# A selective scan whose two products change engines: B to GpSimd, C to VectorE

## The chip, the cores and the metric

The kernel runs on one core of a Trainium2 chip. Its time is device microseconds of one launch, from three runs: a median of 15,365.76 us, between 15,361.5 and 15,403.47. All data is float32.

A core has five engines that run side by side and meet at semaphores: TensorE (PE in the profile), VectorE (DVE), ScalarE (ACT), GpSimd (POOL) and SyncE (SP), which here issues nearly all DMA transfers. Each engine works through its own instructions in order. SBUF is the working memory of 128 partitions; PSUM is the smaller memory that PE writes, and that VectorE and ScalarE, but not GpSimd, read and write in this kernel.

## The reference

Sixteen images of 192 channels and 32 x 32 pixels pass through four layers. The change lies in the third, a selective scan in four directions, with 384 inner channels and 16 states for each channel. Cut to what matters:

```python
def step(h, xs_t):
    d_t, u_t, B_t, C_t = xs_t
    dA = jnp.exp(d_t[..., None] * A)                       # decay
    h = h * dA + (d_t * u_t)[..., None] * B_t[:, :, None, :]
    y = jnp.einsum('bkdn,bkn->bkd', h, C_t)                # sum over the 16 states
    return h, y
```

It runs over the 1024 pixels in each direction k: row by row (0), column by column (1), and both from the end (2 and 3). B and C depend on the pixel, the state and the direction, not on the channel.

## The kernel before

**Units.** The first layer runs ahead of everything else and takes some 3,090 us. The rest, class LayersB, is built around one long sequence of scans. A unit is one scan over 128 partitions x 1024 pixels: 16 channels (CW) times 8 states (NBL). So a group of 16 channels takes two units (BLOCKS = 2), a direction 24 groups or 48 units (DIR_UNITS), an image 192 units (UNITS), and the sixteen images 3072.

**Work of a unit.** With dl (the step d, spread over the states), du (d times u), bb (B) and cb (C) in SBUF:

- `inputs_up` (L1849): once a group, ScalarE copies du into a PSUM buffer xt.
- `decay` (L1853): dA = exp(dl x A), ScalarE, into SBUF; three buffers.
- `inputs` (L1860): xt = xt x bb, VectorE, PSUM to PSUM. Both products of a group are made at its first unit.
- `scan` (L1869): h = scan(dA, xt), VectorE, into SBUF; two buffers. For directions 2 and 3 all views are reversed.
- `outputs` (L1881): hc = h x cb, GpSimd, SBUF to SBUF; three buffers. In directions 1 and 3 the pixels of h stand column by column, and hc is written through a turned view, so that it stands row by row: successive elements go 32 words apart.
- `sums` (L1902 to L1911): PE adds hc over the states with the 0/1 matrix sel, into the PSUM bank acc; after eight units `collect` (L1921) copies acc to y on ScalarE.

**Transfers.** SP issues them all: dl and du for a group (`load_group`, L1816), each 512 KB written by reading one row of a channel eight times; bb and cb for a direction (`load_states`, L1809).

**Order.** Everything from the first scan on is issued in an order written out by `scans`: it walks over slots t = 0 to 191 of each image, and in each slot issues a fixed sequence: products and scan of unit t, the product with C of unit t-1, the sums of unit t-2, the copy of du in odd slots, the decay of unit t+2 (AHEAD), and the transfers that `fetch` finds due. In the room left it puts pieces of other work: `front` (the steps dl and du of the next directions: dlh, duh), and two streams of pieces, `prepare` for the next image and `complete` for the one before (layers 1, 2's ends and 3: convolutions on PE, copies and activations on ScalarE, products on GpSimd). Their instructions appear under L800, the helper that meters them.

A planner decides how many pieces fit. It keeps a clock for each engine, advances VectorE's by SLOT in each slot (4.83 us and 2.31 us in turn) and lets another engine run over the slot's end by OVER; ALLOW is the PE and VectorE work that pieces may bring a slot. A piece marked "late" (a Gelu or Tanh, for which ScalarE loads another function table) goes into odd slots only, at their end. `ln_exp` (L72) loads the table for exp and log again.

**Buffers.** [...]In SBUF lie seventeen buffers of 128 x 1024: dA 3, h 2, hc 3, dl 2, du 2, bb 2, cb 3.

Of the kernel before, what the change touches and what calls it, by code (L numbers as in the profile page):

```python
# [20 lines left out]
L = H * W  # L21
# [746 lines left out]
AHEAD = 2  # L768
# [3 lines left out]
SLOT = (4.83, 2.31)  # L772
OWN = {"POOL": 2.36, "SUMS": 0.6, "START": 0.9, "INPUTS": 1.0, "DECAY": 1.15, "COLLECT": 0.57}
ENGINES = ("PE", "ACT", "POOL", "DVE")
ALLOW = {"PE": 2.45, "DVE": 0.3}
OVER = {"PE": (0.8, 1.2), "ACT": (0.0, 1.5), "POOL": (0.5, 1.5)}
# [38 lines left out]
class Stream:  # L815
# [9 lines left out]
    def step(self):  # L825
        self.engine, lag, *mark = next(self.pieces, (None, 0))
        self.ready = self.at + lag
        self.late, self.piped = "late" in mark, "piped" in mark
        if self.late and self.ready % BLOCKS == 0:
            self.ready += 1  # L830
# [7 lines left out]
    def open(self, t):  # L838

        return self.engine and self.ready <= t and not (self.late and t % BLOCKS != BLOCKS - 1)  # L840


class LayersB:
# [135 lines left out]
    def setup_scans(self):  # L979
# [55 lines left out]
        self.dA, self.h, self.hc = ring("dA", 3, [128, L]), ring("h", 2, [128, L]), ring("hc", 3, [128, L])  # L1035
        self.dl, self.du = ring("dl", 2, [128, L]), ring("du", 2, [128, L])
        self.bb, self.cb = ring("bb", BLOCKS, [128, L]), ring("cb", 3, [128, L])
# [3 lines left out]
        self.xt = [self.xp.tile([128, L], F32, name="xt%d" % i) for i in range(2)]  # L1041
# [108 lines left out]
    def prepare(self, b):  # L1150
# [192 lines left out]
        yield "ACT", 0, "late"  # L1343
        xx = xg if b else self.xx
        for g in range(3):
            nc.scalar.activation(xx[:, g, :], xg[:, g, :], AF.Gelu, bias=self.dw2b[:, g : g + 1])
# [8 lines left out]
        for gs in ((0, 1), (2,)):  # L1355
            zs = [self.p4([128, L], "z") for g in gs]
            for g, z in zip(gs, zs):
                for hf in range(2):
                    yield "PE", 3 if g == 2 and hf == 0 else 0
                    p = self.mm()  # L1360
                    matmuls(
                        nc, p, [(wz[:, i, g * 128 : (g + 1) * 128], x[:, i, half(hf)]) for i in range(2)]
                    )
                    yield "ACT", 0
                    nc.scalar.copy(z[:, half(hf)], p)
            yield "ACT", 0, "late"
            for g, z in zip(gs, zs):
                nc.scalar.activation(z, z, AF.Gelu)
                nc.sync.dma_start(self.zd[one(b), g].rearrange("o p l -> p (o l)"), z)
            cx.ln_exp()  # L1370
# [5 lines left out]
    def complete(self, b):  # L1376
# [8 lines left out]
        if last:  # L1385
            for g in range(3):
                nc.sync.dma_start(self.dA[g], self.zd[b, g])
                nc.sync.dma_start(self.xx[:, g, :], self.yd[g])
        wout = self.weight(I["out_projT"].rearrange("(g p) o -> p g o", p=128), [128, 3, C], "wc", 1)
        for hf in range(2):  # L1390
# [28 lines left out]
            zs = [self.dA[g][:, half(hf)] if last else self.slot("cz", [128, HL], "zh", 3) for g in range(3)]  # L1419
# [30 lines left out]
        for k in range(len(todo) + 2):  # L1450
            if k < len(todo):
                n, r, a = todo[k]
                yield "POOL", 0, "piped"
                t = self.c4([P6, L], "t")
                ts.append(t)
                xa = x[:, a, :]
                tr, xr = (q.rearrange("p (h w) -> p h w", w=W) for q in (t, xa))
                if r == 0:
                    products.tensor_mul(t, xa, xa)
                elif r < 8:  # L1460
                    o = 4 * r * W
                    products.tensor_mul(t[:, o:], xa[:, o:], xa[:, : L - o])
                    products.tensor_mul(t[:, :o], xa[:, :o], xa[:, L - o :])
                else:
                    o = 4 * (r - 7)
                    products.tensor_mul(tr[:, :, o:], xr[:, :, o:], xr[:, :, : W - o])
                    products.tensor_mul(tr[:, :, :o], xr[:, :, :o], xr[:, :, W - o :])
            if 1 <= k <= len(todo):
                yield "ACT", 0, "late", "piped"
                nc.scalar.activation(ts[k - 1], ts[k - 1], AF.Tanh, scale=NS**-0.5)  # L1470
            if k >= 2:
                n, r, a = todo[k - 2]
                yield "PE", 0, "piped"
                for q in range(4):
                    nc.tensor.matmul(
                        ps[32 * q : 32 * q + 32, 0:256], lhsT=self.row[:, NS - n : NS - n + 32],
                        rhs=ts[k - 2][:, 256 * q : 256 * q + 256], start=(k == 2), stop=(k == len(todo) + 1),
                    )
# [74 lines left out]
        for hf in range(2):  # L1553
# [57 lines left out]
            yield "ACT", 0, "late"  # L1611
# [24 lines left out]
    def scans(self, b, more, carry):  # L1636
# [9 lines left out]
        for t in range(UNITS):  # L1646
# [3 lines left out]
            for s in (self.before, self.after):  # L1650
                while s.engine == "ACT" and not s.late and self.fits(s, now + SLOT[t % BLOCKS]):
                    self.advance(s)
            if t % BLOCKS == 0:
                for u in range(t, t + BLOCKS):
                    self.inputs(u)
            self.scan(t)
            clock["DVE"] += SLOT[t % BLOCKS]
            end = now + SLOT[t % BLOCKS]
            if t > 0 or carry:
                self.outputs((t - 1) % UNITS, t == 0)  # L1660
                clock["POOL"] += OWN["POOL"]
            if t > 1 or carry:
                self.sums((t - 2) % UNITS)
            if t % BLOCKS == BLOCKS - 1 and (more or t + 1 < UNITS):
                self.inputs_up((t + 1) % UNITS)
                clock["ACT"] += OWN["INPUTS"]
            if more or t + AHEAD < UNITS:
                self.decay((t + AHEAD) % UNITS)
                clock["ACT"] += OWN["DECAY"]
            if t > 1 or carry:  # L1670
                self.collect((t - 2) % UNITS)
            self.fetch(t, more, carry)
# [24 lines left out]
        if not more:  # L1697
            while self.before.engine:
                self.advance(self.before)
            self.outputs(UNITS - 1)  # L1700
            for u in (UNITS - 2, UNITS - 1):
                self.sums(u)
            self.collect(UNITS - 1)

    def fits(self, s, end):
# [4 lines left out]
        if s.engine != "DVE":  # L1710
            end += OVER[s.engine][self.slots % BLOCKS]
# [18 lines left out]
    def begin(self):  # L1730

        for at, piece in self.front(0):
            if at < 0:
                piece()
        for blk in range(BLOCKS):
            self.load_states(self.bb[blk], 0, blk * NBL)
            self.load_states(self.cb[blk], 0, N + blk * NBL)
        self.turns = 0
        for n in range(2):
            self.load_group(n)  # L1740
        for u in range(AHEAD):
            self.decay(u)
        self.inputs_up(0)
        self.load_group(2)
# [66 lines left out]
    def load_group(self, n):  # L1811
# [3 lines left out]
        for t, src in ((self.dl[n % 2], self.dld), (self.du[n % 2], self.dud)):  # L1815
            self.nc.sync.dma_start(  # L1816
                t, src[k, g, i * CW : (i + 1) * CW, :].unsqueeze(1).to_broadcast([CW, NBL, L])
            )

    def fetch(self, t, more, carry):  # L1820


        n, blk = divmod(t, BLOCKS)
        k, at = divmod(t, DIR_UNITS)
        if more or k + 1 < K:


            if at == DIR_UNITS - 2:
                for i in range(BLOCKS):
                    self.load_states(self.bb[i], (k + 1) % K, i * NBL)  # L1830
            if at == DIR_UNITS - 14:
                self.load_states(self.c_of(k + 1, 0), (k + 1) % K, N)
            if at == DIR_UNITS - 1:
                self.load_states(self.c_of(k + 1, 1), (k + 1) % K, N + NBL)

        due = {DIR_UNITS - 3: (), DIR_UNITS - 2: (n - 1,)}.get(at, (n,) if blk == BLOCKS - 1 else ())
        for n in due:
            if more or n + 3 < K * GROUPS:
                self.load_group((n + 3) % (K * GROUPS))

    def c_of(self, k, blk):

        return self.cb[(2 * (self.turns + k) + blk) % 3]

    def inputs_up(self, u):


        n = u // BLOCKS % 2
        self.nc.scalar.copy(self.xt[n], self.du[n])  # L1849

    def decay(self, u):
        n, blk = divmod(u, BLOCKS)
        self.nc.scalar.activation(  # L1853
            self.dA[u % 3], self.dl[n % 2], AF.Exp, scale=self.A[:, blk, n : n + 1]
        )

    def inputs(self, u):

        n, blk = divmod(u, BLOCKS)
        self.nc.vector.tensor_mul(self.xt[(n + 1 + blk) % 2], self.xt[n % 2], self.bb[blk])  # L1860

    def scan(self, u):
        nc = self.nc
        n, blk = divmod(u, BLOCKS)
        k = n // GROUPS
        views = [self.h[u % 2], self.dA[u % 3], self.xt[(n + 1 + blk) % 2]]
        if k >= 2:
            views = [v[:, ::-1] for v in views]
        nc.vector.tensor_tensor_scan(*views, 0.0, op0=ALU.mult, op1=ALU.add)  # L1869

    def outputs(self, u, carried=False):

        n, blk = divmod(u, BLOCKS)

        k = n // GROUPS - K * (carried and u == UNITS - 1)
        views = [self.hc[u % 3], self.h[u % 2], self.c_of(k, blk)]
        if n // GROUPS % 2:
# [3 lines left out]
        self.nc.gpsimd.tensor_mul(*views)  # L1881
# [145 lines left out]
```

## Time and profile before

| what | value |
|---|---|
| median of three runs | 15,365.76 us |
| span of the profiled execution, first to last instruction | 15,414.4 us |
| scan stage in it, first product to end of last scan | 3,310.2 to 15,273.8 us |
| units in the stage | 3072 |

The profiled execution has no time of its own but its span; it lies 48.6 us above the median of the runs. Its page has, for each group of instructions, the line, the engine, output<-inputs with their shapes and the count; then busy time in all and the mean of one in ns; then the idle time of the engine just before them, and which instruction's end ended most of it. A list of waits has one line for each pair of waiter and releaser: the time in all, how often, and the longest. An answer on one tile or line gives the shortest, median and longest of its instructions.

### The profile page before, as it was taken

How to read it: one execution, taken by the hardware profiler on the slowest of the kernel's cores; microseconds unless marked ns; L12 is line 12 of the kernel's file. 1: busy time of each engine (PE TensorE's matmuls, PEld its weight loads, DVE VectorE, ACT ScalarE, POOL GpSimd, SP SyncE). 2: the span in 40 equal slices, each digit the busy share in tenths (PEclk: the TensorE clock that was granted, in tenths of full speed). 3: DMA queues.
4: the chain of work that ended last, by engine and by line, in shares of the span. 5: the costliest groups of instructions: out<-in, count | busy, mean ns of one | idle time of the engine just before them, and what ended most of it. 6: DMA issues, size and time to landing. Idle time of an engine off the chain costs nothing.

```text
span 15414.4 us, 184312 instructions
## 1 busy us (share of the span) xinstructions
PE 12384.4 (80%) x65856; PEld 4810.3 (31%) x65856; DVE 12329.6 (80%) x10115; ACT 9160.4 (59%) x11881; POOL 10313.5 (67%) x6314
## 2 busy tenths in 40 slices
PE   8999999977777778777778787787878787878755
PEld 4444444422222222222222222222222222222212
DVE  4444444469988988888898989898988888889897
ACT  3333333345666666666666666666666666666665
POOL 2222222237787878787887878787878787878785
PEclk9999999978878887888888888887878787878766
DMA  1000000047878777878777777777777777777774
GB/s 30 15 15 15 17 15 15 14 126 185 214 181 212 185 207 182 208 180 210 189 203 191 199 195 198 195 198 194 197 196 194 195 197 199 194 200 186 200 182 129
DMA packets 884782, 2412.09 MB, mean 156 GB/s; under 512 B 146672, under 2 KB 266944, under 8 KB 876224
## 3 DMA queue, kind: packets, MB, share of 16 engines
q1 hardware_dynamic: 871168, 2397.50, 60.8%
q8 instruction: 532, 8.72, 0.2%
q10 hardware_dynamic: 12736, 3.04, 0.1%
q14 instruction: 346, 2.83, 0.1%
HBM read 2019.10 MB, written 364.30 MB: 155 GB/s over the span
## 4 chain that ended last, share of the span: by engine, by line
PE 19%; DVE 16%; POOL 14%; issue 13%; DMA 10%; ACT 7%; SPq 1%; DVEq 0%; POOLq 0%; ACTq 0%
PE mm L800 15%; DVE h L1869 10%; POOL hc L1881 9%; DVE xt L1860 5%; DMA dl<-dld 3%; PE acc L1911 3%; DMA du<-dud 2%; POOL t L800 2%; ACT dA L1853 2%; ACT xt L1849 2%; DMA y<-ydram 1%; DMA yh<-yd 1%; POOL dlh L800 1%; PE acc L1902 1%; DMA yd<-y 1%
## 5 line engine op out<-in xcount | busy, mean ns | idle before, releaser
L1881 POOL TENSOR_TENSOR hc<-h,cb 128x1024 f32<-128x1024 f32 x3072 | 7245.8, 2371 | 2087.6 <-DVE h L1869 1591.0
L1869 DVE TENSOR_TENSOR_SCAN h<-dA,xt 128x1024 f32<-128x1024 f32 x3072 | 6914.6, 2274 | 299.1 <-POOL hc L1881 292.0
L1860 DVE TENSOR_TENSOR xt<-xt,bb 128x1024 f32<-128x1024 f32 x3072 | 3633.2, 1227 | 904.0 <-ACT xt L1849 771.3
L1853 ACT ACTIVATE dA<-dl,A 128x1024 f32<-128x1024 f32 x3072 | 3507.3, 1146 | 810.3 <-DMA dl<-dld 703.4
L1911 PE MATMUL acc<-hc,sel 128*32 128x256 f32 x24576 | 2406.9, 473 | 1717.2 <-POOL hc L1881 1714.3
L800 PE MATMUL mm<-pad,dg 128*128 128x512 f32 (+1 forms) x5580 | 2911.4, 657 | 13.3 <-ACT pad L800 10.6
L1849 ACT COPY xt<-du 128x1024 f32<-128x1024 f32 x1536 | 1557.8, 1014 | 1350.9 <-DVE h L1869 1163.1
L627 POOL TENSOR_TENSOR D<-D,mask 128x256 f32<-128x256 f32 x768 | 542.7, 738 | 2101.1 <-DVE D L624 2101.1
L1911 PEld LDWEIGHTS acc<-hc,sel 128*32 128x32 f32 x24576 | 561.8, 120 | 4060.2 <-POOL hc L1881 2905.2
L800 PEld LDWEIGHTS mm<-pad,dg 128*128 128x128 f32 (+1 forms) x5580 | 999.1, 193 | 1491.8 <-issue 1370.3
L800 PE MATMUL mm<-x,wgt 96*128 96x512 f32 (+1 forms) x1664 | 1053.7, 769 | 146.8 <-ACT o L800 56.4
L1902 PE MATMUL acc<-y,ident 128*128 128x512 f32 x576 | 442.3, 859 | 447.3 <-ACT y L1921 445.9
L800 POOL TENSOR_TENSOR t<-x 96x768 f32<-96x768 f32 (+4 forms) x510 | 647.3, 1289 | 216.9 <-PE mm L800 216.8
L800 PE MATMUL mm<-d,xT 128*96 128x256 f32 x2048 | 567.9, 415 | 5.4 <-ACT o L800 5.0
L800 POOL TENSOR_TENSOR duh<-dlh,xx 128x512 f32<-128x512 f32 x384 | 537.6, 1400 | 30.1
L800 POOL TENSOR_TENSOR dlh<-dlh,e 128x512 f32<-128x512 f32 x384 | 488.5, 1272 | 103.0 <-ACT e L800 101.0
L800 PEld LDWEIGHTS mm<-x,wgt 96*128 96x128 f32 (+1 forms) x1664 | 339.3, 224 | 672.1 <-issue 363.5
L800 PE MATMUL mm<-xd,dtw 12*128 12x512 f32 x768 | 535.6, 783 | 10.3 <-ACT z L800 10.3
L391 PE MATMUL pc<-ypad,w_c 128*64 128x512 f32 (+1 forms) x1152 | 480.3, 664 | 74.2 <-PEq L751 41.5
L624 DVE SCALAR_TENSOR_TENSOR D<-D,s 128x256 f32<-128x256 f32 x768 | 272.0, 416 | 255.2 <-ACT D L620 255.2
L620 ACT ACTIVATE D<-s 128x256 f32<-128x256 f32 x768 | 233.4, 390 | 338.2 <-PE s L613 332.5
L800 PEld LDWEIGHTS mm<-d,xT 128*96 128x96 f32 x2048 | 328.0, 174 | 261.0 <-issue 164.0
(321 smaller groups left out, 14487.7 us busy)
## 6 DMA issues: line engine op xcount, KB each, us to landing
dl<-dld SPq DMA_DIRECT2D x1536, 512.0 KB
du<-dud SPq DMA_DIRECT2D x1536, 512.0 KB
dld<-dlh SPq DMA_DIRECT2D x384, 256.0 KB
dud<-duh SPq DMA_DIRECT2D x384, 256.0 KB
bb<-xdr SPq DMA_DIRECT2D x128, 512.0 KB
cb<-xdr SPq DMA_DIRECT2D x128, 512.0 KB
dg<-dqd SPq DMA_DIRECT2D x270, 192.0 KB
zd<-z SPq DMA_DIRECT2D x48, 512.0 KB
```

The costliest lines, as they stand in the source:

```text
L391: nc.tensor.matmul(p[r, :], lhsT=w_, rhs=v, start=(n == 0), stop=(n == 14))
L620: nc.scalar.activation(d, S[j][:, two], AF.Exp)
L624: nc.vector.scalar_tensor_tensor(d, d, 2.0, S[j][:, 2 * CH :], op0=ALU.min, op1=ALU.mult)
L627: nc.gpsimd.tensor_mul(d, d, mask)
L800: return f(out, *args, **kw)
L1849: self.nc.scalar.copy(self.xt[n], self.du[n])
L1853: self.nc.scalar.activation(self.dA[u % 3], self.dl[n % 2], AF.Exp, scale=self.A[:, blk, n : n + 1])
L1860: self.nc.vector.tensor_mul(self.xt[(n + 1 + blk) % 2], self.xt[n % 2], self.bb[blk])
L1869: nc.vector.tensor_tensor_scan(*views, 0.0, op0=ALU.mult, op1=ALU.add)
L1881: self.nc.gpsimd.tensor_mul(*views)
L1902: nc.tensor.matmul(acc, lhsT=self.cx.ident, rhs=self.y[:, g, half(pair)], start=True, stop=False)
L1911: nc.tensor.matmul(self.acc[rows4(q), q4(s)], lhsT=self.sel[:, m, :], rhs=self.hc[u % 3][:, q4(q)], start=False, stop=(s + m + blk == 3),)
```

## The change

The two products of a unit change places and engines, and with them the memories:

- `inputs`: xs = du x bb on GpSimd, SBUF to SBUF, for unit t+2 in slot t; three buffers xs. The copy of du (`inputs_up`) is gone.
- `decay`: written into PSUM, into one of two buffers h, for unit t+1 in slot t.
- `scan`: in place in PSUM, from h and xs into h.
- `outputs`: hc = h x cb on VectorE, straight behind the scan of the same unit, with the same turned view of hc in directions 1 and 3.
- `sums` and `collect` follow one slot after the scan in place of two.
- `fetch`: dl is loaded two groups ahead and du three, both in even slots; bb has three buffers as cb has, and the loads of a new direction go out 14 and 4 slots (bb) or 14 and 2 (cb) ahead of it.
- `late` is gone: Gelu and Tanh may go into any slot, and each Gelu is a piece of its own.
- Planner: SLOT is 3.55 in every slot; ALLOW for PE 2.7 in place of 2.45; OVER for PE 2.5, ACT 1.0, POOL 2.5.

The seventeen SBUF buffers are now xs 3, hc 3, dl 2, du 3, bb 3, cb 3. The output stage of the last image, which used dA as space, uses xs.

The core of the diff:

```diff
-AHEAD = 2
-SLOT = (4.83, 2.31)
+SLOT = 3.55
+EARLY = 1.3
-ALLOW = {"PE": 2.45, "DVE": 0.3}
-OVER = {"PE": (0.8, 1.2), "ACT": (0.0, 1.5), "POOL": (0.5, 1.5)}
+ALLOW = {"PE": 2.7, "DVE": 0.3}
+OVER = {"PE": 2.5, "ACT": 1.0, "POOL": 2.5}
...
-        self.dA, self.h, self.hc = ring("dA", 3, [128, L]), ring("h", 2, [128, L]), ring("hc", 3, [128, L])
-        self.dl, self.du = ring("dl", 2, [128, L]), ring("du", 2, [128, L])
-        self.bb, self.cb = ring("bb", BLOCKS, [128, L]), ring("cb", 3, [128, L])
+        self.xs, self.hc = ring("xs", 3, [128, L]), ring("hc", 3, [128, L])
+        self.dl, self.du = ring("dl", 2, [128, L]), ring("du", 3, [128, L])
+        self.bb, self.cb = ring("bb", 3, [128, L]), ring("cb", 3, [128, L])
-        self.xt = [self.xp.tile([128, L], F32, name="xt%d" % i) for i in range(2)]
+        self.h = [self.xp.tile([128, L], F32, name="h%d" % i) for i in range(2)]
...
-        yield "ACT", 0, "late"
         xx = xg if b else self.xx
         for g in range(3):
+            yield "ACT", 0
             nc.scalar.activation(xx[:, g, :], xg[:, g, :], AF.Gelu, bias=self.dw2b[:, g : g + 1])
...
                 while s.engine == "ACT" and self.fits(s, now + EARLY - OVER["ACT"]):
                     self.advance(s)
-            if t % BLOCKS == 0:
-                for u in range(t, t + BLOCKS):
-                    self.inputs(u)
+            if more or t + 1 < UNITS:
+                self.decay((t + 1) % UNITS)
+            if more or t + 2 < UNITS:
+                self.inputs(t + 2)
             self.scan(t)
+            self.outputs(t)
             if t > 0 or carry:
-                self.outputs((t - 1) % UNITS, t == 0)
-            if t > 1 or carry:
-                self.sums((t - 2) % UNITS)
-            if t % BLOCKS == BLOCKS - 1 and (more or t + 1 < UNITS):
-                self.inputs_up((t + 1) % UNITS)
-            if more or t + AHEAD < UNITS:
-                self.decay((t + AHEAD) % UNITS)
-            if t > 1 or carry:
-                self.collect((t - 2) % UNITS)
+                self.sums((t - 1) % UNITS)
+                self.collect((t - 1) % UNITS)
...
     def fetch(self, t, more):
         k, at = divmod(t, DIR_UNITS)
         if more or k + 1 < K:
+            for tiles, o, first, second in ((self.bb, 0, 14, 4), (self.cb, N, 14, 2)):
+                for blk, lead in enumerate((first, second)):
+                    if at == DIR_UNITS - lead:
+                        self.load_states(self.turn_of(tiles, k + 1, blk), (k + 1) % K, o + blk * NBL)
+        n, blk = divmod(t, BLOCKS)
+        for tiles, src, lead in ((self.dl, self.dld, 2), (self.du, self.dud, 3)):
+            if blk == 0 and (more or n + lead < K * GROUPS):
+                self.load_group(tiles, src, (n + lead) % (K * GROUPS))
...
     def decay(self, u):
         n, blk = divmod(u, BLOCKS)
         self.nc.scalar.activation(
-            self.dA[u % 3], self.dl[n % 2], AF.Exp, scale=self.A[:, blk, n : n + 1]
+            self.h[u % 2], self.dl[n % 2], AF.Exp, scale=self.A[:, blk, n : n + 1]
         )
     def inputs(self, u):
         n, blk = divmod(u, BLOCKS)
-        self.nc.vector.tensor_mul(self.xt[(n + 1 + blk) % 2], self.xt[n % 2], self.bb[blk])
+        self.nc.gpsimd.tensor_mul(self.xs[u % 3], self.du[n % 3], self.turn_of(self.bb, n // GROUPS, blk))
     def scan(self, u):
+        h, x = self.h[u % 2], self.xs[u % 3]
+        if u // DIR_UNITS >= 2:
+            h, x = h[:, ::-1], x[:, ::-1]
+        self.nc.vector.tensor_tensor_scan(h, h, x, 0.0, op0=ALU.mult, op1=ALU.add)
     def outputs(self, u):
+        k, at = divmod(u, DIR_UNITS)
+        views = [self.hc[u % 3], self.h[u % 2], self.turn_of(self.cb, k, at % BLOCKS)]
+        if k % 2:
             views = [views[0].rearrange("p (h w) -> p w h", w=W)] + [
                 v.rearrange("p (w h) -> p w h", h=H) for v in views[1:]
             ]
-        self.nc.gpsimd.tensor_mul(*views)
+        self.nc.vector.tensor_mul(*views)
```

## The prediction

> **What bounds the kernel now.** I read the page's busy shares and groups first, then the list of waits, then busy time over the scan stage, then the rows that show what an access pattern costs.
>
> ```profile
> span 15414.4 us, 184312 instructions
> PE 12384.4 (80%) x65856; PEld 4810.3 (31%) x65856; DVE 12329.6 (80%) x10115; ACT 9160.4 (59%) x11881; POOL 10313.5 (67%) x6314
> L1881 POOL TENSOR_TENSOR hc<-h,cb 128x1024 f32<-128x1024 f32 x3072 | 7245.8, 2371 | 2087.6 <-DVE h L1869 1591.0
> L1869 DVE TENSOR_TENSOR_SCAN h<-dA,xt 128x1024 f32<-128x1024 f32 x3072 | 6914.6, 2274 | 299.1 <-POOL hc L1881 292.0
> L1860 DVE TENSOR_TENSOR xt<-xt,bb 128x1024 f32<-128x1024 f32 x3072 | 3633.2, 1227 | 904.0 <-ACT xt L1849 771.3
> L1853 ACT ACTIVATE dA<-dl,A 128x1024 f32<-128x1024 f32 x3072 | 3507.3, 1146 | 810.3 <-DMA dl<-dld 703.4
> L1849 ACT COPY xt<-du 128x1024 f32<-128x1024 f32 x1536 | 1557.8, 1014 | 1350.9 <-DVE h L1869 1163.1
> ```
>
> There are 3072 units of scan (16 images, 4 directions, 48 units); each takes one product and one scan on VectorE. The stage runs from the first product at 3310.2 us to the end of the last scan at 15273.8 us: 11,964 us, or 3.89 us a unit. In it:
>
> ```profile
> 3300.00:15280.00 11980.00, 9224.59 (x42538) 3215.64 (x42536) 10738.85 (x7134) 7896.55 (x9517) 9529.57 (x5246) 0.80 0.77 195
> ```
>
> After the length come PE, PEld, VectorE, ScalarE, GpSimd, the clock, DMA share and GB/s. VectorE is busy for 10,739 us (90%), GpSimd 80%, PE 77%, ScalarE 66%. VectorE sets the pace; its idle time is 11,964 - 10,739 = 1,225 us. Whom it waits for, over the same stretch:
>
> ```profile
> DVE xt L1860 <- ACT xt L1849: 771.3, 364, 30.0
> DVE h L1869 <- POOL hc L1881: 292.0, 233, 3.4
> DVE yh L800 <- PE mm L800: 40.7, 16, 5.0
> ```
>
> So 1,225 us is the most that a better order can give; the rest is VectorE's own work.
>
> **Copy and decays.** The 1536 copies of du go: 1,558 us of ScalarE, none of VectorE. What counts is the 771 us that VectorE waited for them. A copy could start when the even scan ended and had to be done when the odd scan ended: slack 2.27 - 1.01 = 1.26 us. Now the decay takes that place, for it writes the h buffer that the product of unit t-1 has just read, and scan t+1 needs it: slack 2.27 + 1.23 - 1.15 = 2.35 us, more where the product is slower. The mean overrun was 771/364 = 2.1 us; some 1.1 us more of slack takes about half of it. Against that, every unit is exposed instead of every second, and behind a late ScalarE stand the decay and the copy of acc, for which VectorE and PE wait. If overruns fall off exponentially with a mean of 2.1 us, the share kept is exp(-1.1/2.1) = 0.6, so 771 us becomes 460 us with the same number of chances and 920 us with twice as many. ScalarE loses 0.5 us of work a unit and the dl transfers get more lead (below), so I take the lower, with 40 us for the waits on PE: **500 us** of idle time, ends 200 and 1,000. The decay itself may be 1.01 (the copy that wrote PSUM) to 1.15 us; VectorE's work covers it, unless it is late.
>
> **Product with B on GpSimd.** 3072 products of the shape, type and memory of L1881, now all contiguous, replace L1881's: 7,246 us, nothing net. It is issued two slots ahead into three buffers, so a GpSimd piece has to run over a whole slot before VectorE notices; I count the 292 us wait as gone. It waits for scan t-1, du and bb; the pieces of the other images (dlh, duh, t, D) queue behind it, and their stores dld and dud on SP.
>
> **Scan in place.** 2.27 us as now. The scan of L1869 reads PSUM and SBUF; no row has a scan that writes PSUM, but L1860 writes PSUM in 1.23 us while L131 does the same work wholly in SBUF in 1.22. Between 0 and 0.03 us a unit (92 us); I take 0.
>
> **Product with C on VectorE.** It takes the place of the product with B, 1.23 us: nothing net where it is contiguous. But in directions 1 and 3, half of the units, it writes hc through a turned view: neighbours in the stream lie 32 words apart. GpSimd hardly notices (median 2360 ns in a direction 0, 2381 in the direction 1 after it):
>
> ```profile
> L1881 POOL TENSOR_TENSOR hc<-h,cb x43: 2339/2360/2389, 7073.4 to 7233.6; 128x1024 f32<-128x1024 f32 x43
> L1881 POOL TENSOR_TENSOR hc<-h,cb x42: 2362/2381/2399, 7261.2 to 7413.5; 128x1024 f32<-128x1024 f32 x42
> ```
>
> No VectorE row in the trace writes so. Two rows are near: ScalarE's copies of xd, alternately contiguous and turned with the same step, and a small reduction of VectorE that reads 96 elements at that step, against one of 4 elements (min/median/max):
>
> ```profile
> L800 ACT COPY xd<-mm x1: 578/578/578, 3283.9 to 3283.9; 44x512 f32<-44x512 f32 x1
> L800 ACT COPY xd<-mm x2: 578/816/1055, 3283.9 to 3284.5; 44x512 f32<-44x512 f32 x2
> ...
> L231 DVE TENSOR_REDUCE row<-ident x1: 315/315/315, 5.1 to 5.1; 128x24 f32<-128x96 f32 x1
> L238 DVE TENSOR_REDUCE rowg<-ident x6: 145/146/146, 5.3 to 5.7; 128x1 f32<-128x4 f32 x6
> ```
>
> ScalarE: (1014 - 578)/512 = 0.85 ns an element contiguous, and (1055 - 578)/512 = 0.93 more turned: 1.78 ns. VectorE reading: (315 - 146)/92 = 1.84 ns. Two engines of different speed end at about 1.8 ns, so I take 1.8 for VectorE's write, against (1227 - 667)/512 = 1.09 contiguous (667 is its 512-wide yh row), or 1.04 at the least: 1024 x 0.75 = **0.77 us** a product, 1536 x 0.77 = 1,183 us. The Trainium skill (Vector Engine (DVE) Microarchitecture Reference, Measured stream behaviour on trn2) speaks against the change: a port keeps its rate only on runs of two adjacent words, and a destination alone costs 1.71 ns an element hopping 4 KiB and 2.50 to 2.51 stepping 24 words, against 1.05. By its ends the product grows by 0.68 or 1.49 us, 1,040 or 2,290 us in all. I keep these as ends, and the rows for the value, as they have the very step.
>
> **Transfers.** Same number and size of dl, du, bb and cb. A load of dl went out behind the decay at the end of an odd slot, for a decay after the next long and short slot: 2 x 1.23 + 2.27 + 2.27 = 7.0 us on. Now it goes out some 1.2 us into an even slot for a decay at the start of the third slot after: 3 x 3.5 - 1.2 = 9.3 us. That is 2.3 us more lead, against 703 us of ScalarE waiting for dl. du has a third buffer; its issue now waits for GpSimd, on SP behind dl, with the stores dld and dud behind both. Loads of bb move from 2 slots ahead to 14 and 4. DMA stands at 77%, so nothing on the path; a gain is within the idle time above.
>
> **Table loads.** Without "late", Gelu and Tanh may go in any slot, one by one. Now there are 197 pairs of loads in the stage (13 an image); at the most 26 an image if each of 18 Tanh and 8 Gelu has its own, 195 pairs more. The row is
>
> ```profile
> L72 ACT ACT_TABLE_LOAD x197 | 252.8, 1283 | 3.5
> ```
>
> and in the order of time the next activation starts 1.29 us after a load, so a pair is 2.57 us and 195 of them 500 us of ScalarE. The Trainium skill (ScalarE: Activation LUTs, What ACT_TABLE_LOAD costs) adds a drain of some 1.38 us, 2.66 us a load: 1,040 us. By either ScalarE stays under 7,897 - 1,558 + 1,040 = 7,380 us of 12,400: off the path, save for single late decays, which the 500 us hold. I take the row.
>
> **Planner.** The larger PE allowance and the wider overruns order pieces differently; they add no work. PE at 77% and GpSimd at 80% have room, but less than ScalarE in a direction 0, where PE is busy 137.5 of 160 us. The end of the program saves one trailing product, some 2 us.
>
> **Sum.** 10,739 + 1,183 + 500 = 12,422 us of stage against 11,964: +458 us. Against the profiled span that is 15,872; the span is 49 us over the median of the runs, so on the median 15,366 + 458 = **15,824 us**, 3.0% slower. The gain in waits is real (725 us) and smaller than the turned write.
>
> **Rivals.**
> - The turned write costs VectorE little, as it costs GpSimd. Then the waits decide: 10,739 + 500 - 11,964 = -725, 14,640 us. It turns at 725/1536 = 0.47 us a product: faster below. Against it: both near rows lie at 0.75 or above. 12%.
> - The turned write costs the skill's 1.49 us: 10,739 + 2,290 + 400 (long slots leave more slack) = 13,429, 16,830 us. For it: 24 words is near 32; against it: the 1.84 ns of VectorE's own read. 18%.
> - ScalarE's one-slot lead fails: its waits on PE and dl reach VectorE nearly every time, idle 1,000 us: 12,922, 16,325 us. For it: ScalarE works in order, and waited 370 us for PE at pad alone. 12%.
> - Loss and gain cancel: 0.68 us and idle 200: 11,984, 15,390 us. 8%, of which half within 0.3%, a quarter on each side.
> - The likeliest, 15,550 to 16,150: 50%.
>
> **How the numbers follow.** A measurement of this kernel can tell about 0.3%, 46 us. Faster: 12 + 2, less 1 for a write between the cases, 13%; within: 4 + 1, 5%; slower: 82%. The range leaves out the first rival, the faster part of the fourth and the far end of the second: 15,340 to 16,950.
>
> **What would show it.** The product on VectorE in two populations, near 1.23 us and 2.0 us, the second in directions 1 and 3 alone, with those directions near 4.3 us a unit and the others near 3.7; scan at 2.27; GpSimd's product at 2.36; VectorE waiting for decays in place of the copy, some 500 us in all; no wait for GpSimd worth naming. Wrong: a single population of products near 1.23 (the first rival), or directions 0 and 2 not under 3.89 us.

## The result and the profile after

The changed kernel takes 15,890.93 us (median of four runs, 15,883.45 to 15,927.11) against 15,363.63 us for the kernel before on the same chip: a ratio of 1.034, 95% interval 1.0325 to 1.0358. It is slower by 3.4%; 15,824 us and 3.0% were forecast.

The page of the kernel after, busy shares and the groups of the scan:

```profile
span 15886.6 us, 183427 instructions
PE 12436.4 (78%) x65856; PEld 4818.6 (30%) x65856; DVE 13489.8 (85%) x10115; ACT 7815.3 (49%) x10376; POOL 10309.3 (65%) x6314
L1837 POOL TENSOR_TENSOR xs<-du,bb 128x1024 f32<-128x1024 f32 x3072 | 7240.9, 2362 | 2549.1 <-DVE h L1844 2313.6
L1844 DVE TENSOR_TENSOR_SCAN h<-h,xs 128x1024 f32<-128x1024 f32 x3072 | 7019.1, 2285 | 216.1 <-ACT h L1830 174.2
L1830 ACT ACTIVATE h<-dl,A 128x1024 f32<-128x1024 f32 x3072 | 3428.6, 1117 | 4601.1 <-DVE hc L1854 4146.4
L1854 DVE TENSOR_TENSOR hc<-h,cb 128x1024 f32<-128x1024 f32 x3072 | 4856.9, 1581 | 319.0 <-DVE h L1844 7.8
```

The scan, the decay and GpSimd's product last about what they did. VectorE's product has a mean of 1,581 ns where the product with B had 1,227. That mean is of two populations, as the answers on the tile hc show, first in a direction 1 or 3, then in a direction 0 or 2 (shortest/median/longest):

```profile
L1854 DVE TENSOR_TENSOR hc<-h,cb x10: 1918/1950/1984, 5879.8 to 5917.5; 128x1024 f32<-128x1024 f32 x10
L1854 DVE TENSOR_TENSOR hc<-h,cb x11: 1223/1225/1225, 6080.5 to 6118.1; 128x1024 f32<-128x1024 f32 x11
```

Over the scan stage, busy times in the order PE, PEld, VectorE, ScalarE, GpSimd, and whom VectorE waits for in it:

```profile
3306.00:15750.00 12444.00, 9274.78 (x42526) 3226.67 (x42526) 11899.54 (x7134) 6540.92 (x8002) 9520.32 (x5244) 0.78 0.74 188
```
```profile
DVE h L1844 <- ACT h L1830: 174.2, 134, 6.7
DVE h L1844 <- POOL xs L1837: 41.4, 8, 31.7
DVE yh L800 <- PE mm L800: 27.0, 11, 5.5
```

The stage grew from 11,964 to 12,444 us. VectorE's busy time grew by 1,161 us and its idle time fell from 1,225 to 544. The wait for ScalarE is down from 771 to 174 us, the wait for GpSimd from 292 to 41. Only some 250 us of the idle time is put down to another engine; the remaining 300 us lie in front of the product with C (319.0 us in its row, 16 of them put down to something), a tenth of a microsecond each time. The forecast has no such term. The order of time shows it, VectorE alone (start, duration), in a turned direction and in a straight one:

```profile
5881.65 2.29 DVE L1844 TENSOR_TENSOR_SCAN h<-h,xs 128x1024 f32<-128x1024 f32 x1
5884.04 1.96 DVE L1854 TENSOR_TENSOR hc<-h,cb 128x1024 f32<-128x1024 f32 x1
5885.82 2.31 DVE L1844 TENSOR_TENSOR_SCAN h<-h,xs 128x1024 f32<-128x1024 f32 x1
...
6081.67 2.29 DVE L1844 TENSOR_TENSOR_SCAN h<-h,xs 128x1024 f32<-128x1024 f32 x1
6084.06 1.23 DVE L1854 TENSOR_TENSOR hc<-h,cb 128x1024 f32<-128x1024 f32 x1
6085.21 2.29 DVE L1844 TENSOR_TENSOR_SCAN h<-h,xs 128x1024 f32<-128x1024 f32 x1
```

and in the kernel before, where VectorE waits for no other engine (two instructions merged in a line):

```profile
15262.52 4.46 DVE L1869 TENSOR_TENSOR_SCAN h<-dA,xt 128x1024 f32<-128x1024 f32 x2
15267.08 2.37 DVE L1860 TENSOR_TENSOR xt<-xt,bb 128x1024 f32<-128x1024 f32 x2
15269.35 4.46 DVE L1869 TENSOR_TENSOR_SCAN h<-dA,xt 128x1024 f32<-128x1024 f32 x2
```

Before, a pair of units takes 15,269.35 - 15,262.52 = 6.83 us, 3.415 a unit. After, a straight unit takes 6,085.21 - 6,081.67 = 3.54 us, for the product starts 0.1 us after its scan has ended (6,084.06 against 6,081.67 + 2.29), where other instructions start a little before their predecessor's end. The kernel before has this gap too, but once in two units: the first product of a pair starts at 15,267.08, the scan before it ended at 15,262.52 + 4.46 = 15,266.98. That product overwrites the buffer xt that the scan just before it has read, and in the trace a wait on VectorE's own counter stands ahead of it. Of the 904 us of idle time in its row some 791 are put down to something, so about 113 us of such gaps were there before the change, against 300 now.

A turned unit takes 4.17 us: 0.63 us more, not the 0.72 us that the durations differ by, for the next scan starts 0.18 us before a turned product's recorded end and only 0.08 us before a straight one's.

### The profile page after: what moved, and what is told of

It is laid out like the page before. It is cut to its first block, busy times and chain, and to the rows that moved or that the text cites. A ratio compares the mean times of both kernels' runs of the same rounds, so it can differ in the third digit from the quotient of the medians.

```text
span 15886.6 us, 183427 instructions
## 1 busy us (share of the span) xinstructions
PE 12436.4 (78%) x65856; PEld 4818.6 (30%) x65856; DVE 13489.8 (85%) x10115; ACT 7815.3 (49%) x10376; POOL 10309.3 (65%) x6314
## 5 line engine op out<-in xcount | busy, mean ns | idle before, releaser
L1837 POOL TENSOR_TENSOR xs<-du,bb 128x1024 f32<-128x1024 f32 x3072 | 7240.9, 2362 | 2549.1 <-DVE h L1844 2313.6
L1844 DVE TENSOR_TENSOR_SCAN h<-h,xs 128x1024 f32<-128x1024 f32 x3072 | 7019.1, 2285 | 216.1 <-ACT h L1830 174.2
L1830 ACT ACTIVATE h<-dl,A 128x1024 f32<-128x1024 f32 x3072 | 3428.6, 1117 | 4601.1 <-DVE hc L1854 4146.4
L1854 DVE TENSOR_TENSOR hc<-h,cb 128x1024 f32<-128x1024 f32 x3072 | 4856.9, 1581 | 319.0 <-DVE h L1844 7.8
L800 PE MATMUL mm<-x,wgt 96*128 96x512 f32 (+1 forms) x1664 | 1110.4, 803 | 146.4 <-ACT o L800 43.2
L1875 PE MATMUL acc<-y,ident 128*128 128x512 f32 x576 | 407.4, 797 | 82.0 <-ACT y L1894 82.0
L1894 ACT COPY y<-acc 128x512 f32<-128x512 f32 x384 | 224.1, 584 | 317.2 <-PE acc L1884 313.0
```

The costliest lines, as they stand in the source:

```text
L800: return f(out, *args, **kw)
L1830: self.nc.scalar.activation(self.h[u % 2], self.dl[n % 2], AF.Exp, scale=self.A[:, blk, n : n + 1])
L1837: self.nc.gpsimd.tensor_mul(self.xs[u % 3], self.du[n % 3], self.turn_of(self.bb, n // GROUPS, blk))
L1844: self.nc.vector.tensor_tensor_scan(h, h, x, 0.0, op0=ALU.mult, op1=ALU.add)
L1854: self.nc.vector.tensor_mul(*views)
L1875: nc.tensor.matmul(acc, lhsT=self.cx.ident, rhs=self.y[:, g, half(pair)], start=True, stop=False)
```

## The experiments

**The turned write taken away.**

```diff
-        if k % 2:
-            views = [views[0].rearrange("p (h w) -> p w h", w=W)] + [
-                v.rearrange("p (w h) -> p w h", h=H) for v in views[1:]
-            ]
         self.nc.vector.tensor_mul(*views)
```

> The changed kernel, but hc is written straight in all four directions; the turn back to row order is left out, so directions 1 and 3 are summed with their columns unturned. Theory (the turned write costs VectorE 0.71 us a product in 1536 units): the product is 1.23 us everywhere, 1,098 us of VectorE's work go, and 50 to 250 us of waits for ScalarE come, because slots are shorter: 14,850 to 15,050 us, which is faster than the kernel before by 2 to 3.5%. Rival (the new order with one slot's lead for the decay is what costs, and the turned write only fills time in which VectorE would wait): the time falls by less than 500 us, to 15,400 or more, and VectorE waits for decays for over 700 us.

Measured: 15,175.72 us, 0.986 of the kernel before (0.984 to 0.988). That is 715 us less than the changed kernel (the kernel before took 15,389 us beside it, 26 more than beside the changed one). The direction was the theory's, and the rival, which needed 15,400 or more, falls; but the theory's range is missed too, by 126 us. Stage and waits:

```profile
3312.00:15060.00 11748.00, 9110.28 (x42518) 3186.41 (x42518) 10934.64 (x7134) 6520.69 (x8002) 9494.51 (x5243) 0.80 0.78 199
```
```profile
DVE h L1844 <- ACT h L1830: 385.1, 254, 7.7
DVE hc L1850 <- PE acc L1880: 38.8, 28, 3.2
```

VectorE is busy 965 us less than with the turn, 0.63 us for each of the 1536 products, not 0.71: I had taken the difference of the recorded durations. And idle time rose from 544 to 813 us, since shorter slots leave ScalarE less slack. So all of the change but the turned write is worth 11,964 - 11,748 = 216 us of stage, and the turned write takes 696. Those 216 us hold the copy's going, the new order, the planner's new numbers and the earlier loads together; no run parts them.

**The suspected cost doubled.**

```diff
-        if k % 2:
+        if True:
             views = [views[0].rearrange("p (h w) -> p w h", w=W)] + [
```

> The changed kernel with the suspected cost doubled: hc is written turned in all four directions, so directions 0 and 2 are summed with rows and columns exchanged. Theory: 1536 more products of 1.94 us: +1,098 us of VectorE's work, less 50 to 150 us of waits that the longer slots hide: 16,840 to 16,940 us. Rival (the turned write is partly hidden, or the order is what costs): under 16,500 us.

Measured: 16,706.67 us, 1.086 of the kernel before (1.084 to 1.087); 816 us more than the changed kernel. The rival, under 16,500, falls; the theory's range is missed from below, again for the 0.63 us:

```profile
3314.00:16577.00 13263.00, 9529.13 (x42523) 3294.99 (x42526) 12871.38 (x7134) 6553.51 (x8002) 9539.61 (x5244) 0.77 0.69 176
```

| scan stage, us | before | straight | changed | all turned |
|---|---|---|---|---|
| length | 11,964 | 11,748 | 12,444 | 13,263 |
| VectorE busy | 10,739 | 10,935 | 11,900 | 12,871 |
| VectorE idle | 1,225 | 813 | 544 | 392 |
| of it, waiting for ScalarE's copy or decay | 771 | 385 | 174 | 58 |

Two steps of 1536 turned products add 965 and 972 us of busy time. Over these three kernels the cost is linear, and what the longer slots give back is idle time.

**The disputed cost by itself.** For the views, step(t, s) takes elements s words apart, and rows_(t, s) is the same loop over contiguous data.

```diff
+        for _ in REP:
+            nc.vector.tensor_mul(step(out, 32), rows_(h, 32), rows_(cb, 32))
...
+        for _ in REP:
+            nc.vector.tensor_mul(rows_(out, 32), step(h, 32), rows_(cb, 32))
```

> The changed kernel with 64 more instructions behind its end, four of each kind, every engine on its own: products of 1024 elements on VectorE (PSUM times SBUF, into SBUF) whose output steps 1, 2, 4, 8, 16, 24, 32 and 64 words from element to element, or goes in pairs of neighbours 32 words apart; with the PSUM input or the SBUF input turned in place of the output; with a turned output in PSUM; a ScalarE copy straight and turned; a GpSimd product straight and turned. Theory (a port slows where single words follow each other, whatever the step): 1.23 us for step 1 and for the pairs, 1.9 to 2.0 for every step from 2 or 4 on, 1.9 to 2.0 for a turned SBUF input, ScalarE 1.0 and 1.9, GpSimd 2.36 and 2.38. By the figures of the Trainium skill (Vector Engine (DVE) Microarchitecture Reference, Measured stream behaviour on trn2) step 24 should be near 2.6 us and far steps near 1.8. Rival (the memory's banks decide): 32 and 64 words much slower than 8 or 24. Turned PSUM operands: between 1.23 and 2.0 us, not known. The whole takes some 130 us more.

Measured: 15,938.38 us in a single run, 47 us above the changed kernel where some 130 were expected, for the new instructions ran between the last image's pieces. So the engines were not each on its own, though GpSimd stood idle beside all steps from 1 to 64 words. Four instructions of each kind (shortest/median/longest, ns). In order: output steps 1, 2, 4, 24 (1008 elements) and 32 words; pairs 32 words apart; PSUM input turned; SBUF input turned; PSUM output turned; ScalarE's copy straight and turned; GpSimd's product straight and turned:

```profile
L933 DVE TENSOR_TENSOR hc<-h,cb x4: 1203/1216/1225, 15761.5 to 15766.9; 128x1024 f32<-128x1024 f32 x4
L935 DVE TENSOR_TENSOR hc<-h,cb x4: 1224/1224/1225, 15768.1 to 15771.9; 128x1024 f32<-128x1024 f32 x4
L937 DVE TENSOR_TENSOR hc<-h,cb x4: 1970/1984/1992, 15773.2 to 15782.2; 128x1024 f32<-128x1024 f32 x4
L943 DVE TENSOR_TENSOR hc<-h,cb x4: 2502/2558/2562, 15813.2 to 15820.9; 128x1008 f32<-128x1008 f32 x4
L945 DVE TENSOR_TENSOR hc<-h,cb x4: 1883/1940/1948, 15823.5 to 15851.1; 128x1024 f32<-128x1024 f32 x4
L949 DVE TENSOR_TENSOR hc<-h,cb x4: 1214/1223/1225, 15861.0 to 15865.0; 128x1024 f32<-128x1024 f32 x4
L951 DVE TENSOR_TENSOR hc<-h,cb x4: 1215/1224/1225, 15870.9 to 15874.6; 128x1024 f32<-128x1024 f32 x4
L953 DVE TENSOR_TENSOR hc<-h,cb x4: 1943/1947/1951, 15875.9 to 15881.8; 128x1024 f32<-128x1024 f32 x4
L955 DVE TENSOR_TENSOR h<-h,cb x4: 1217/1232/1233, 15883.7 to 15887.5; 128x1024 f32<-128x1024 f32 x4
L957 ACT COPY hc<-h x4: 1001/1012/1012, 15888.8 to 15892.4; 128x1024 f32<-128x1024 f32 x4
L959 ACT COPY hc<-h x4: 1867/1930/1941, 15893.5 to 15903.4; 128x1024 f32<-128x1024 f32 x4
L961 POOL TENSOR_TENSOR hc<-xs,cb x4: 2338/2341/2342, 15905.4 to 15914.1; 128x1024 f32<-128x1024 f32 x4
L963 POOL TENSOR_TENSOR hc<-xs,cb x4: 2363/2365/2382, 15917.1 to 15924.5; 128x1024 f32<-128x1024 f32 x4
```

Every other word is free, pairs of neighbours 32 words apart are free, and from 4 words on single words cost: 2.0 us at 4 and 8 words, 1.9 at 16, 32 and 64, 2.56 at 24 (medians not shown above: 1,996 ns at 8, 1,876 at 16, 1,903 at 64). So the rival of the banks falls: 32 and 64 words are no slower than 8. The Trainium skill's figure for a step of 24 words (Vector Engine (DVE) Microarchitecture Reference, Measured stream behaviour on trn2: 2.50 to 2.51 ns an element) is nearly met, with 2.56 us for 1008 elements or 2.54 ns each. But it does not carry over to 32 words, near as that is, and one number "whatever the step", as I had it, is wrong too. The same turn costs nothing where VectorE reads or writes PSUM. ScalarE pays as VectorE does; GpSimd, at 2.3 ns an element anyway, pays 0.02 us.

**The turn on TensorE.** The summing matmuls read hc in any case; here they read it turned. This kernel computes everything.

```diff
+        hc = self.hc[u % 3]
         for q in range(4):
+            x = hc[:, q4(q)] if k % 2 == 0 else hc.rearrange("p (w h) -> p h w", h=H)[:, 8 * q : 8 * q + 8, :]
             nc.tensor.matmul(
-                self.acc[rows4(q), q4(s)], lhsT=self.sel[:, m, :], rhs=self.hc[u % 3][:, q4(q)],
+                self.acc[rows4(q), q4(s)], lhsT=self.sel[:, m, :], rhs=x,
```

> As the straight kernel, but complete: in directions 1 and 3 PE's summing matmuls read hc turned, 32 words from one column to the next. Theory (only VectorE's and ScalarE's ports pay for single words[...]; a float32 matmul takes 403 ns for 256 columns, 1.57 ns each, and so has little to lose): matmuls of 0.40 to 0.46 us, time within 100 us of the straight kernel, 14,850 to 15,150 us, faster than the kernel before. Rival (PE pays too, 1.8 ns a column on top): 0.85 us a matmul, 4 x 0.45 = 1.8 us more PE work a unit in half of the units, with PE busy three quarters of the time: 15,500 us or more.

Measured: 15,242.94 us, 0.991 of the kernel before (0.989 to 0.994), 67 us above the straight kernel; of the two profiled executions it is 17 us the longer (15,213.2 and 15,196.7). TensorE pays in part: the matmuls of a straight and of a turned direction, then all summing matmuls without the turn and with it,

```profile
L1882 PE MATMUL acc<-hc,sel x124: 379/403/636, 5879.5 to 5936.9; 128*32 128x256 f32 x124
L1882 PE MATMUL acc<-hc,sel x128: 379/607/636, 6080.1 to 6138.9; 128*32 128x256 f32 x128
...
L1880 PE MATMUL acc<-hc,sel 128*32 128x256 f32 x24576 | 2385.8, 468 | 1777.1 <-DVE hc L1850 1761.5
L1882 PE MATMUL acc<-hc,sel 128*32 128x256 f32 x24576 | 2736.6, 526 | 1659.5 <-DVE hc L1850 1646.5
```

take 0.40 and 0.61 us, between the 0.46 of the theory and the 0.85 of the rival. They overlap: 24,576 of 526 ns would be 12.9 ms one after another, and keep PE busy for 2.74 ms. So their busy time grows by only 351 us, and PE's in the whole stage by 200, from 9,110 to 9,310 out of 11,762; other matmuls got shorter, beside a granted clock of 0.82 in place of 0.80. The time is outside the theory's range, as the straight kernel's is, and well under the rival's bound; the distance to the straight kernel is as expected.

**Reading turned from PSUM.**

```diff
-            views = [views[0].rearrange("p (h w) -> p w h", w=W)] + [
-                v.rearrange("p (w h) -> p w h", h=H) for v in views[1:]
-            ]
+            views[1] = views[1].rearrange("p (w h) -> p h w", h=H)
+            views[0], views[2] = (views[i].rearrange("p (h w) -> p h w", w=W) for i in (0, 2))
```

> The changed kernel, but in directions 1 and 3 VectorE reads h turned from PSUM and writes hc straight; C is taken as it lies, unturned, so these directions are summed with C's pixels in column order. Theory (single words cost at SBUF's ports and not at PSUM's, as the products on their own showed: 1.22 us for a turned PSUM input against 1.94 for a turned SBUF output): products of 1.23 us everywhere and the straight kernel's time within 60 us, 15,115 to 15,235. Rival (PSUM's turned read is free only where PE and ScalarE leave PSUM alone): products above 1.4 us, 15,400 or more.

Measured: 15,191.39 us, 0.987 of the kernel before (0.985 to 0.988), all products between 1,223 and 1,227 ns. The theory holds inside the loop too, with PE and ScalarE at work on PSUM. Used for the real sum it would need C in row order, which this kernel does not prepare.

**The product ahead of the scan.** This takes from the straight kernel the product's dependence on the instruction just before it.

```diff
+            self.outputs(t)
             self.scan(t)
-            self.outputs(t)
```

> The straight kernel with the product with C ahead of the scan of its unit in place of behind it: it then multiplies the decays by C and leaves the scan's result out of the output. Every instruction and buffer stays; only the product no longer reads what the instruction just before it wrote. Theory (a VectorE instruction that needs its predecessor's output starts 0.12 us later than one that doesn't: 3.54 us a unit in the straight kernel against 3.415 in the kernel before): 3072 x 0.12 = 370 us less, with up to 100 us of it lost to waits for ScalarE, 14,780 to 14,920 us. Rival (the gap belongs to the scan that writes PSUM in place, or to switching between the two kinds of instruction): within 60 us of the straight kernel's 15,176.

Measured: 14,917.45 us, 0.969 of the kernel before (0.968 to 0.971), 258 us less than the straight kernel. It is just inside the range's upper end, and the trace shows that the theory holds for half of the units only. A direction run forwards, and one run from the end:

```profile
5593.71 2.28 DVE L1844 TENSOR_TENSOR_SCAN h<-h,xs 128x1024 f32<-128x1024 f32 x1
5595.90 1.20 DVE L1850 TENSOR_TENSOR hc<-h,cb 128x1024 f32<-128x1024 f32 x1
5597.03 2.28 DVE L1844 TENSOR_TENSOR_SCAN h<-h,xs 128x1024 f32<-128x1024 f32 x1
...
6080.51 2.30 DVE L1844 TENSOR_TENSOR_SCAN h<-h,xs 128x1024 f32<-128x1024 f32 x1
6082.72 1.21 DVE L1850 TENSOR_TENSOR hc<-h,cb 128x1024 f32<-128x1024 f32 x1
6084.03 2.30 DVE L1844 TENSOR_TENSOR_SCAN h<-h,xs 128x1024 f32<-128x1024 f32 x1
```

From scan to scan it is 5,597.03 - 5,593.71 = 3.32 us forwards and 6,084.03 - 6,080.51 = 3.52 us reversed; the straight kernel had 3.54 in both. Here the product reads the very buffer that the scan behind it overwrites. A forward scan writes in the order in which the product reads; a reversed one writes first what the product reads last. In the program the reversed scans, and only they, carry a wait on VectorE's own counter for the instruction just before; in the straight kernel nearly every product carries one, in the kernel before the first product of each pair. (The scans of the kernel before carry one as well, on a product two instructions back.) With no such wait, one in two units and one in each, a unit takes 3.32, 3.415 and 3.54 us. So the wait for the instruction just before costs some 0.2 us a time. Over 1536 forward units that is 1536 x 0.22 = 338 us, of which 258 reached the time; in the stage the wait for the decay went from 385 to 371 us, that for PE's sum, now in front of the product, from 39 to 79, and the rest is not accounted for.

```profile
3299.00:14782.00 11483.00, 8916.15 (x42530) 3162.82 (x42530) 10758.37 (x7134) 6515.69 (x8005) 9496.04 (x5245) 0.81 0.80 204
```

VectorE's busy time is back at 10,758 us, where the kernel before had 10,739: both carry such a wait in about half of the units. That also says what "busy" held in the straight kernel's 10,935: instructions that no longer overlap at their ends. The rival, no more than 60 us from the straight kernel, falls.

**The kernel before without its copy.** This asks whether the copy alone could have been dropped. du is read from SBUF in the product on VectorE, and is loaded two groups ahead.

```diff
-            if t % BLOCKS == BLOCKS - 1 and (more or t + 1 < UNITS):
-                self.inputs_up((t + 1) % UNITS)
-                clock["ACT"] += OWN["INPUTS"]
...
+        if blk == 0 and (more or t // BLOCKS + 2 < K * GROUPS):
+            self.load_group((t // BLOCKS + 2) % (K * GROUPS), (1,))
...
-        self.nc.vector.tensor_mul(self.xt[(n + 1 + blk) % 2], self.xt[n % 2], self.bb[blk])
+        self.nc.vector.tensor_mul(self.xt[(n + 1 + blk) % 2], self.du[n % 2], self.bb[blk])
```

> The kernel before with one part of the change alone: the copy of du is gone, and VectorE multiplies du by bb straight from SBUF into xt; du is loaded two groups ahead in even slots. Theory (VectorE shares a read path of SBUF with GpSimd, so a product with two SBUF inputs and GpSimd's product, busy 80% of the time, hold each other up; Trainium skill, SBUF — State Buffer, Who interferes with whom): VectorE's product grows from 1.23 to 2 us or more, GpSimd's from 2.37 to 3 or more; 16,500 to 19,000 us. That would be why the change keeps one operand of each VectorE instruction in PSUM. Rival (no such contention, for VectorE's product of two SBUF inputs in the first layer takes 1.22 us): the 771 us of waits for the copy go, 14,600 to 15,000 us.

Measured: 19,399.87 us, 1.261 of the kernel before (1.258 to 1.263), beyond the theory's upper end of 19,000 and far from the rival. The groups of the page, then GpSimd and VectorE in order of time (two products merged in each line):

```profile
L1879 POOL TENSOR_TENSOR hc<-h,cb 128x1024 f32<-128x1024 f32 x3072 | 8514.5, 2785 | 3906.9 <-DVE h L1867 2797.1
L1858 DVE TENSOR_TENSOR xt<-du,bb 128x1024 f32<-128x1024 f32 x3072 | 7097.4, 2353 | 192.3 <-DMA du<-dud 135.0
```
```profile
8004.00 5.63 POOL L1879 TENSOR_TENSOR hc<-h,cb 128x1024 f32<-128x1024 f32 x2
8006.00 4.73 DVE L1858 TENSOR_TENSOR xt<-du,bb 128x1024 f32<-128x1024 f32 x2
```

With both inputs in SBUF the product has a mean of 2.35 us where it had 1.23, and GpSimd's product beside it 2.79 where it had 2.37; VectorE's was as expected, GpSimd's a little under the 3 us or more. The 141 products beside which GpSimd did nothing have a median of 1.22 us, the other 2,931 one of 2.19: the two engines hold each other up. VectorE is busy for 14,201 us in the stage, 3,460 more, and in 18 places waits for a decay, 886 us together (the longest 74.9). The Trainium skill (SBUF — State Buffer, Who interferes with whom) has the rule, that a VectorE instruction with two SBUF inputs contends with a GpSimd instruction that reads SBUF; this trace agrees, and here it costs a quarter of the kernel. So the product could not have dropped the copy and stayed on VectorE: moving it to GpSimd and putting the decay into PSUM, which gives the scan and the product on VectorE one PSUM input each, belong together.

**ScalarE's slot reordered.** The straight-writing kernel with the turn on TensorE left ScalarE waiting for PE's sum ahead of the decay. Here the copy of that sum goes behind the decay, at the slot's end; everything is computed.

```diff
                 self.sums((t - 1) % UNITS)
-                self.collect((t - 1) % UNITS)
...
+            if t > 0 or carry:
+                self.collect((t - 1) % UNITS)
             self.slots += 1
```

> The kernel with the turn on PE, and the copy of acc issued at the end of ScalarE's slot, behind the other work, in place of right behind the decay. Theory (ScalarE's 528 us of waiting for PE at that copy hold back the next decay, and VectorE behind it): 50 to 150 us less than with the turn on PE alone, 15,090 to 15,190 us. Rival (the wait only moves: PE then waits for the copy before its next group of sums, and the pieces behind it are late): 15,220 us or more.

Measured: 15,156.64 us, 0.984 of the kernel before (0.983 to 0.986), 86 us less than with the copy of the sum in its old place, and within the theory's range. It computes all of the reference and takes 1.6% less than the kernel before and 15,157/15,891 = 0.954 of the changed kernel. From the waits, first with the copy early, then late:

```profile
ACT y L1892 <- PE acc L1882: 528.1, 208, 10.8
DVE h L1844 <- ACT h L1830: 380.9, 274, 8.1
DVE hc L1850 <- PE acc L1882: 52.7, 40, 3.4
```
```profile
ACT y L1893 <- PE acc L1883: 260.2, 133, 9.2
DVE h L1845 <- ACT h L1831: 388.0, 262, 32.6
DVE hc L1851 <- PE acc L1883: 7.8, 8, 1.7
```

ScalarE's wait for PE halves. But VectorE's wait for the decay, through which I expected the gain, did not fall. The gain shows elsewhere: VectorE's wait for PE's sum went from 53 to 8 us, that for GpSimd from 44 to 13. These 76 us compare with the 53 us between the two profiled executions (15,213.2 and 15,160.1), so something else gave part of them back; that, and why GpSimd's share fell, is not settled. The size was right, the path was not.

## Why the prediction was right and where it was wrong

The time was 0.4% above the forecast, and the sign and the main mechanism were right: the turned write outweighs the waits won. That the stage agrees so closely (12,422 us forecast, 12,444 measured) is luck: errors of some 200 to 300 us cancelled.

- **The turned write.** 0.77 us a product and 1,183 us were forecast. The recorded durations differ by 0.72 us, and what VectorE loses is 0.63 us or 965 us: mis-sized by 218 us. Two things are in it: the difference of the durations is 0.70 ns an element where I took 0.75; and a longer record overlaps the next start by more, so durations overstate the loss. To take the rows in place of the 24-word figure was right: that figure of the Trainium skill (Vector Engine (DVE) Microarchitecture Reference, Measured stream behaviour on trn2) would have made it 1.49 us, and step 24 took 2.56 us here where 32 words took 1.94. The lower of the two ends put down, 0.68 us, was nearer than the value.
- **Waits, 500 us.** Measured 174 for the decay, 41 for GpSimd, 27 for PE at yh, some 250: half of what was put down. The estimate took 0.6 of 771 us for a slack 1.1 us longer. Straight, with that slack, 385 us are left, a half; with the turned write 174, for the term "more where the product is slower" was named and not counted. How ScalarE's lead depends on the slot is shown by the three kernels of the new order in the table: 385, 174 and 58 us, straight, changed and all turned.
- **The term left out.** Each product with C reads what the scan just before it wrote and waits for it; of the products with B only the first of each pair had to wait for the scan just before it. In the profile that is about 300 us of idle time ahead of the product, and 10,935 - 10,739 = 196 us more of busy time without the turn. Start to start it is (3.54 - 3.415) x 3072 = 384 us; the two together, 496 us, are 112 more, which matches the 113 us of gaps that the kernel before already had. An estimate from the runs comes out near: 1536 more waits of 0.22 us are 338 us, and the scan's 2,288 - 2,274 = 14 ns in the straight kernel are 43 us in all. The step "It takes the place of the product with B, 1.23 us: nothing net where it is contiguous" failed: the duration is the same, the place in the order is not. Nor was the 1,225 us of idle time the most that a better order could give, for how far instructions overlap at their ends is part of the busy time.
- **Sum.** 12,422 - 218 - 250 + 300 + 196 = 12,450 against 12,444.
- **Nothing net, as forecast.** GpSimd's product 2.362 us (2.371 before), the decay 1.117 (1.01 to 1.15), the scan in place 2.285 (2.274; bounds 0 and 92 us, measured 0.011 x 3072 = 34). The wait for GpSimd is all but gone, 292 to 41. ScalarE's wait for dl fell from 703 to 242 us. Table loads rose from 197 to 211 each way; 195 more were the bound.
- **Directions.** Straight ones were forecast near 3.7 and turned ones near 4.3 us a unit; over all images they took 3.77 and 4.34 on average, from scan to scan.
- **Rivals.** The turned write is not free (0.63 us), and the point at which the change would break even is lower than the 0.47 us put down, since the rest of the change wins 216 us and not 725: 216/1536 = 0.14 us net of the waits given back. ScalarE's lead did not fail, the 1.49 us did not come, and gain and loss did not cancel.

## What to carry to other kernels

When an instruction is exchanged for one of the same length, look at what stands right before it in its engine's order: to wait for the immediate predecessor, for its output or to overwrite what it reads, cost some 0.2 us a time. The mean durations do not show it, and one such wait a unit in place of one in two made 384 us, 2.5% of the time. Cost an access pattern from start to start in the loop, at its own step and in its own memory: the same transpose was 0.63 us a time on VectorE's write to SBUF, free from and to PSUM, and 17 to 67 us in all where TensorE read it. And when an engine is freed of a copy, ask which memory the operand comes from then: dropped from the kernel before by itself, the copy would have cost 26%.

## What the runs showed of the hardware that was not expected

- A VectorE instruction that waits for the one just before it starts 0.1 us after that one's end, and without the wait 0.08 to 0.1 us before it: 3.54 us against 3.32 for a product and a scan.
- VectorE's turned access (32 words) costs in SBUF alone: 1.94 us written, 1.95 us read, against 1.22 us; from and to PSUM 1.22 and 1.23 us.
- The cost is not monotonic in the step: 1.22 us at 2 words, 1.98 at 4, 2.56 at 24 (for 1008 elements), 1.94 at 32; pairs of neighbours 32 words apart 1.22.
- ScalarE's copy writes turned in 1.93 us against 1.01, GpSimd's product in 2.37 against 2.34.
- TensorE's fp32 matmul of 256 columns takes 0.61 us when its moving operand steps 32 words, against 0.40.
- Two SBUF inputs take VectorE's product from 1.23 to 2.35 us beside GpSimd, which itself slows from 2.37 to 2.79.
